# ScalarE copies P1's bank into P2's, and the second level of the ff residual's P5 and P7 in every block

## The chip, the cores and the metric

One NeuronCore of a Trainium2 chip runs the whole program. The metric is device time in microseconds (us) of one execution, lower is better. The engines meant below are TensorE (PE in the profile, PEld for its weight loads), VectorE (DVE), ScalarE (ACT), GpSimd (POOL) and SyncE (SP, which issues most DMAs).

## The reference, cut to what matters

Two sequences of 2048 rows with 512 features pass through one conditioned layer; everything is fp32.

```
emb = silu(t) @ ada_w + ada_b             # 6 rows of 512 per sequence: shift, scale, gate, twice
norm = LN(x) * (1 + scale_msa) + shift_msa
h = gelu(norm @ ssm_w1 + ssm_b1)          # 512 x 512, exact gelu
x = x + gate_msa * (h @ ssm_w2 + ssm_b2)  # 512 x 512
norm2 = LN(x) * (1 + scale_mlp) + shift_mlp
hf = gelu(norm2 @ ff_w1 + ff_b1)          # 512 x 1024, tanh gelu
x = x + gate_mlp * (hf @ ff_w2 + ff_b2)   # 1024 x 512
```

## The kernel before, in words

The 4096 rows are cut into eight blocks of 512 (`NBLK`), four to a sequence (`PER_B`), numbered 0 to 7. The gates are multiplied into the second weights, which is why those weights are folded anew for the second sequence (in the iteration of block 3 and what follows it, "refold").

Matrix products are done by Strassen's method (Winograd's form): 2 by 2 quarters, seven products P1 to P7 instead of eight, with sums of the operands ahead of them and sums of the results behind. Four kinds of products, in the order in which one iteration `i` of the main loop runs them:

- **products** (`Second.products`, tiles `hC_i`): hidden layer of the ff part of block i, a bilinear program of 26 products that is read from a table (`HK_P`). Its banks in PSUM are first taken by ACT (L946) and then added by DVE (L949); gelu is on ACT (L927). It takes 22.45 us of PE.
- **oA_{i+1}** (`residual`, `group`): the ssm residual of the next block, seven products of 1.727 us, 12.09 us together. `group` writes the products in the order ORDER = P1, P2, P6, P5, P7, P3, P4. Products that share a result are accumulated in one bank: BANK puts P1, P6, P7, P4 in bank y, P2 in x, P5 and P3 in v. DVE reads a bank after each product (L697) and adds it into `x`. P6 accumulates on P1 in bank y, and so on, so that the result of P1 is contained in what is read later. Banks y and v are seeded with the bias row by an ACT copy (`seed`, L446).
- **oC_i** (`residual_in_leaves`): the ff residual of block i. P1 and P6 are done plainly (16 passes of 215.9 ns each); P2, P3, P4 by a second level of seven "leaves" each, of 0.447 us. Where `five` is true (blocks 2, 3, 5, 6, 7), P5 and P7 are done by leaves as well, and in blocks 1 and 4 plainly. Leaf r of all five products is done together, the leaf P1 being r=0; DVE adds it from PSUM into `x` (L795).
- **hA_{i+2}** (`First`, `hidden`): hidden layer of the ssm part of the block after next, again seven products in ORDER, results taken by DVE or, for those named in `on_act`, by ACT; gelu on ACT. In blocks with `five` those are P6 and P5, else none.

The operands of Strassen's products need sums: of the hidden values (L348, on POOL, mostly 128x512 or 128x256 tensor_tensor), of the normalised rows ("forms", L870, on POOL) and of the weights of the leaves (`leaves_of_weight`, L348). The last kind is made twice, for each sequence. In block 1 its parts for P2, P3, P4 are on POOL in products 1; the eight instructions for P5 and P7, called `later`, are on DVE (128x256), three in hA_3 and five in products 2. In block 4 all parts are on DVE, after the weights were multiplied by the gate.

The order is written out by hand. Each group of products calls `hooks`: a list of operations put behind each product (by name in `group`, by slot number in `products`, R0 to R6 for the leaves), and an engine runs its instructions in the order in which they are written. Nothing is scheduled by a tool. An operation in a hook thus stands in the queue of its engine in front of all that is written later, whether or not anybody waits for it.

Norm statistics are done on DVE (L508, L509, bn_stats), their scales in eight small POOL instructions (L517 to L535, some 3 us), normalisation on ACT (L549), the transpose on DVE (L560) and DMAs.

## Time and profile before

| | us |
|---|---|
| median of 3 runs (lowest, highest) | 589.98 (589.6, 590.53) |
| the profiled execution | 591.35 |
| its span | 589.2 |
| PE busy | 579.3 (98%) |
| DVE busy | 432.1 (73%) |
| POOL busy | 424.2 (72%) |
| ACT busy | 241.4 (41%) |

The profiled execution's time is 1.37 us above the median; the span is 2.15 us shorter than its own time. Times below are counted from the start of the span. PE starts and ends of stages that the text uses: oA_2 155.56, oC_1 167.65, products 2 202.93, oC_2 237.46, hA_5 329.16, products 4 341.25, oA_5 363.97, oC_4 376.06, products 7 537.72, oC_7 561.63; PE's last matmul ends at 585.17. In the list of instructions by time ("the timeline"), the columns are the start, the busy time, engine, line, operation, what is written from what, shapes, how many run together (x2 is two, with their common busy time), and in brackets the idle time of the engine before it with what ended it. In the list of waits, each line has the waiting instruction, the one waited for, and the total, the number and the longest of the waits.

### The profile page before, as it was taken

Reading aid. Unit: us, or ns where it says so; the run is one execution under the profiler, and the core shown is the slowest. Engines: PE = TensorE matmul, PEld = TensorE weight load, DVE = VectorE, ACT = ScalarE, POOL = GpSimd, SP = SyncE. Lnnn points to the kernel's source line nnn. Section 1 sums busy time; section 2 is a strip of 40 time slices with the busy share of each in tenths; the row PEclk is TensorE's granted clock in tenths of the full one; section 3 lists DMA queues with packets and bytes.
Section 4 is the critical chain, followed back from the end, with each engine's and each line's share of the span. In section 5 each row is a group of like instructions: output and inputs, shape, how many; then the busy total and the mean of one; then the engine's idle time right before and its main releaser. Section 6 shows DMA issues by size and latency. Waiting matters only on the chain.

```text
span 589.2 us, 9347 instructions
## 1 busy us (share of the span) xinstructions
PE 579.3 (98%) x3255; PEld 515.4 (87%) x3255; DVE 432.1 (73%) x784; ACT 241.4 (41%) x417; POOL 424.2 (72%) x509
## 2 busy tenths in 40 slices
PE   7999999999999999999999999999999999999997
PEld 3888888888889888998889988898889988898887
DVE  4979788987755785776757697767767736688686
ACT  2235357405633255434742457114464245322420
POOL 1776259999964958979788769965979792756461
PEclk9999999999999999999999999999999999999999
DMA  8990323403215402462033711423120420013002
GB/s 314 395 389 11 92 59 80 113 19 125 51 23 144 161 0 68 117 205 78 1 90 78 280 71 23 122 49 123 44 54 20 135 81 1 0 40 105 1 1 73
DMA packets 25243, 56.49 MB, mean 96 GB/s; under 512 B 4672, under 2 KB 5740, under 8 KB 23532
## 3 DMA queue, kind: packets, MB, share of 16 engines
q1 hardware_dynamic: 21472, 51.15, 27.3%
q10 hardware_dynamic: 3724, 4.75, 3.3%
q8 instruction: 26, 0.43, 0.3%
q14 instruction: 21, 0.17, 0.1%
HBM read 32.80 MB, written 8.40 MB: 70 GB/s over the span
## 4 chain that ended last, share of the span: by engine, by line
PE 89%; DVE 3%; DMA 2%; POOL 2%; issue 1%; ACTq 1%; ACT 0%; SPq 0%; POOLq 0%; DVEq 0%
PE px_hC L932 10%; PE py_hA L474 9%; PE py_oA L474 9%; PE pv_hC L932 8%; PE py_hC L932 8%; PE py_oC L735 7%; PE pl_oC_P_y L781 6%; PE pv_hA L474 4%; PE pv_oA L474 4%; PE pl_oC_P_v L781 4%; PE py_hC L474 2%; PE px_hA L474 2%; PE px_oA L474 2%; PE py_oC L474 2%; DMA ada<-in_L_cond_ada_w_dram 2%; PE pl_oC_P_x L781 2%
## 5 line engine op out<-in xcount | busy, mean ns | idle before, releaser
L508 DVE BATCH_NORM_STATS2 st<-x 128x6 f32<-128x512 f32 x64 | 43.4, 678 | 6.6 <-DMA x<-in_x_dram 6.4
L348 POOL TENSOR_TENSOR hSC<-hClo,hChi 128x512 f32<-128x512 f32 (+1 forms) x17 | 20.6, 1214 | 37.9 <-ACT hChi L927 19.1
L592 ACT ACTIVATE nT<-nT,mod,mod 128x512 f32<-128x512 f32 x30 | 22.0, 802 | 61.2 <-DMA nT<-blocks 46.5
L870 POOL TENSOR_TENSOR forms<-forms 128x256 f32<-128x256 f32 x55 | 41.4, 752 | 4.7 <-DVE forms L870 1.5
L932 PE MATMUL py_hC<-forms,fw 128*128 128x256 f32 x168 | 40.8, 379 | 0.0
L949 DVE TENSOR_TENSOR hClo<-hClo,py_hC 128x512 f32<-128x512 f32 x42 | 28.6, 684 | 15.4 <-ACT hClo L946 8.6
L549 ACT ACTIVATE nT<-x,nmr,rstd 128x512 f32<-128x512 f32 x32 | 23.4, 803 | 33.3 <-POOL nmr L535 33.3
L932 PEld LDWEIGHTS py_hC<-forms,fw 128*128 128x128 f32 x168 | 31.8, 190 | 4.4
L697 DVE TENSOR_TENSOR x<-py_oA,x 128x512 f32<-128x512 f32 x32 | 22.0, 688 | 18.1 <-PE py_oA L474 16.8
L795 DVE TENSOR_TENSOR x<-pl_oC_P_y,x 128x256 f32<-128x256 f32 (+1 forms) x76 | 28.1, 371 | 9.6 <-PE pl_oC_P_y L781 7.7
L592 ACT ACTIVATE x<-x,mod,mod 128x512 f32<-128x512 f32 x24 | 17.6, 802 | 39.7 <-DMA x<-blocks 39.7
L735 PE MATMUL py_oC<-fw,hClo 128*128 128x256 f32 x144 | 33.5, 379 | 0.0
L870 POOL TENSOR_TENSOR forms<-nT 128x256 f32<-128x256 f32 x12 | 8.9, 742 | 29.9 <-DMA out_dram<-x 10.2
L735 PEld LDWEIGHTS py_oC<-fw,hClo 128*128 128x128 f32 x144 | 26.7, 190 | 3.3
L870 POOL TENSOR_TENSOR forms<-nT,forms 128x256 f32<-128x256 f32 x39 | 28.7, 755 | 1.0 <-DVE forms L870 0.5
L517 POOL TENSOR_SCALAR ve<-mv 128x4 f32<-128x4 f32 x16 | 3.8, 240 | 34.3 <-DVE mv L509 26.1
L949 DVE TENSOR_TENSOR hChi<-hChi,pv_hC 128x512 f32<-128x512 f32 x35 | 23.2, 679 | 7.1 <-PE pv_hC L932 7.0
L927 ACT ACTIVATE hClo<-hClo,colsT 128x256 f32<-128x256 f32 x56 | 25.3, 499 | 6.0 <-DVE hClo L949 5.7
L932 PE MATMUL px_hC<-forms,fw 128*128 128x256 f32 x112 | 27.6, 379 | 0.0
L474 PE MATMUL py_oA<-w,hA 128*128 128x256 f32 x112 | 26.5, 379 | 0.0
L927 ACT ACTIVATE hChi<-hChi,colsT 128x256 f32<-128x256 f32 x56 | 25.1, 497 | 1.9 <-DVE hChi L949 1.9
L946 ACT ACTIVATE hClo<-px_hC 128x512 f32<-128x512 f32 x21 | 12.5, 597 | 32.0 <-PE px_hC L932 25.4
(330 smaller groups left out, 1763.5 us busy)
## 6 DMA issues: line engine op xcount, KB each, us to landing
x<-in_x_dram SPq DMA_DIRECT2D x13, 1024.0 KB
out_dram<-x SPq DMA_DIRECT2D x14, 512.0 KB
ada<-in_L_cond_ada_w_dram SPq DMA_DIRECT2D x6, 1024.0 KB
x<-blocks SPq DMA_DIRECT2D x96, 64.0 KB
nT<-blocks SPq DMA_DIRECT2D x72, 64.0 KB
fw<-in_L_cond_ff_w_dram SPq DMA_DIRECT2D x2, 2048.0 KB
nT<-blocks ACTq DMA_DIRECT2D x56, 64.0 KB
w<-in_L_cond_ssm_w_dram SPq DMA_DIRECT2D x3, 1024.0 KB
```

The source lines that it names most:

```text
L474: nc.tensor.matmul(ps[b][j * apart][:, j, :], lhs(p, j, k), rhs(p, j, k), start=(fresh and j * (not apart) == 0 and k == 0), stop=(p in (" ...
L508: nc.vector.bn_stats(st, xs[self.i][:, c, :])
L549: nc.scalar.activation(t, x_c, AF.Identity, bias=self.nmr[:, c : c + 1], scale=self.rstd[:, c : c + 1])
L592: nc.scalar.activation(dst, src, AF.Identity, bias=shift, scale=scale)
L697: nc.vector.tensor_tensor(d, ps[BANK[p]][:, js], d, ALU.add)
L735: yield lambda j=j, k=k: nc.tensor.matmul(ps[BANK[p]][:, j, :], hops(p, j, k), wops[p][:, k, :], start=False, stop=(k == kdim - 1), skip_g ...
L781: nc.tensor.matmul(t[:, n, :], hops.leaves[p][f][:, k, :], leaf_wops[p][f][:, k, :], start=room not in started, stop=(f in ("P2", "P3", "P ...
L795: nc.vector.tensor_tensor(d, src, d, ALU.add)
L870: eng.tensor_tensor(reg[d], reg[a], reg[b], ALU.add if f == "+" else ALU.subtract)
L927: nc.scalar.activation(h, h, AF.Gelu_apprx_tanh, bias=fb1T[:, m : m + 1])
L932: nc.tensor.matmul(ps[b][:, j, :], fa[ra][:, j * P : (j + 1) * P], fb[rb].rearrange("p a (c q) -> p c a q", q=Q), start=(fresh and j == 0) ...
L949: nc.vector.tensor_tensor(dest(d), dest(d), ps[b], op)
```

## The change

- A second order, CARRIED = P1, P5, P6, P2, P7, P3, P4, is used in residual oA_2 to oA_7 and in hidden hA_3 to hA_7. After P1, ACT copies P1's bank y into bank x, PSUM to PSUM (128x512), and P2 accumulates on the copy. DVE no longer adds P1 on its own; in hA, ACT takes the finished bank x by gelu with the bias. The hooks stay at their positions: the place is that of ORDER (`places`). P6, which writes bank y next, now waits for the copy. `on_act` is P6 and P5 in all of these hA.
- In oC of blocks 1 to 5 and 7 the same is done one level down: after leaf r=0, ACT copies P23's y bank (128x256), P4's y bank (128x256) and the v seed (128x128) into the x banks on which leaf P2 (r=1) accumulates, and DVE's four adds of r=0 are dropped.
- `five` is true in every block, so P5 and P7 are done by leaves in blocks 1 and 4 too, with their sums on POOL.
- `later` of block 1 moves into oA_2: two DVE instructions behind each of its first four products. `apart_leaves` moves from oC to slot 4 of products 1 and 4.
- The refold for the second sequence is spread in another way: seven folds and P23 sums in hA_5, POOL sums of 128x1024 at slots 5 and 8 of products 4, the P4 leaf sums on POOL, P23's last two and two of `later` on DVE in oA_5, the other six of `later` in oC_4.
- The statistics of norm 1 of block 6 move from DVE to ACT: four Identity activations with an accumulated sum in hA_5 and four Square activations in products 4.
- Block 7: `sums24` on DVE, `sums35` and `sums7` on POOL; leaf r=6 in the order P4, P7, P2 and P3, P5. Block 6: the adds of r=5 in the order P5, P4, P7, P3.

```diff
+    CARRIED = ("P1", "P5", "P6", "P2", "P7", "P3", "P4")
@@ group
+            if p == "P1" and order is CARRIED:
+                ps["x"] = [ps_g.tile([P, 2, HT], F32, tag="x", name=f"px_{name}_0")]
+                nc.scalar.copy(ps["x"][0], ps["y"][0])
-            for op in hooks.get(p, ()):
+            for op in hooks.get(place, ()):
@@ Norm
+        def sums_on_act(self):
...
+                nc.scalar.activation(
+                    self.unread[:, c], xs[self.i][:, c, :], AF.Identity, scale=1.0 / D, accum_out=self.mv[:, c, :1]
+                )
+        def squares_on_act(self):
...
+                nc.scalar.activation(
+                    self.unread[:, c], xs[self.i][:, c, :], AF.Square, bias=less[:, c : c + 1], accum_out=self.mv[:, c, 1:]
+                )
@@ hidden
             if p == "P1":
-                take_first(p, s1, ps["y"], 0)
+                if order is not CARRIED:
+                    take_first(p, s1, ps["y"], 0)
+            elif p == "P2" and order is CARRIED:
+                for j in range(2):
+                    nc.scalar.activation(s1[:, j], ps["x"][:, j], func, bias=bT[:, m0 + j : m0 + j + 1])
@@ residual
+            if p == "P1" and order is CARRIED:
+                return
@@ residual_in_leaves
+            if last and r == 6:
+                on = ("P4", "P7", "P2", "P3", "P5")
...
+            if r == 0 and carried:
+                x23, x4 = rooms["P23", "x"], rooms["P4", "x"]
+                nc.scalar.copy(x23[:, :2], rooms["P23", "y"][:, :2])
+                nc.scalar.copy(x4[:, : 1 + five], rooms["P4", "y"][:, : 1 + five])
+                if five:
+                    nc.scalar.copy(x4[:, 2], seeded[:, 0])
+                started |= {("P23", "x"), ("P4", "x")}
+                dests = {}
+            for p in ("P5", "P4", "P7", "P3") if i + 2 == NBLK and r == 5 else on:
@@ main loop, products
-        five = i % PER_B != (1 if i < PER_B else 0)
+        five = True
-            hook(hooks, (0, 1, 3, 5, 7), later)
+            hook(hooks, (1, 1, 3, 5, 7), unread_stats)
-            hook(hooks, (0, 0, 1), fold[:3])
-            hook(hooks, (9,), fold[3:7])
+            hook(hooks, (0,), fold[:1])
+            hook(hooks, (5, 8), fold[1:5])
+            hook(hooks, (8, 13), fold[5:7])
+            hook(hooks, (13,), fold[9:13])
+            hook(hooks, (4,), [lambda: apart_leaves(gb[5], nc.gpsimd)])
@@ main loop, oA and oC
-        engs = (nc.gpsimd, nc.gpsimd, nc.gpsimd if nx2 else nc.vector)
+        engs = (nc.vector if last else nc.gpsimd, nc.gpsimd, nc.gpsimd if nx2 or last else nc.vector)
+            if i == 1:
+                hook(hooks, ("P1", "P1", "P2", "P2", "P6", "P6", "P5", "P5"), later)
-                hook(hooks, ("P1", "P2", "P6", "P5"), fold[7:11])
+                hook(hooks, ("P1", "P2", "P6", "P5"), fold[8:9] + fold[7:8] + later[:2])
-            residual(f"oA_{i + 1}", i + 1, hA[i + 1], w2_ops, KD // 2, hooks)
+            residual(f"oA_{i + 1}", i + 1, hA[i + 1], w2_ops, KD // 2, hooks, order=CARRIED)
+            hook(hooks, ("P1", "R0") if leaf_fold else ("P1", "P1", "R0") if nx2 else ("P1",), [lambda c=c: n2[i + 1].normal(c) for c in range(C)])
+                hook(hooks, ("P1",), leaf_fold[2:])
@@ main loop, hA
-            hook(hooks, ("P5", "P5", "P7", "P3", "P4"), fold[:5])
+            hook(hooks, ("P5", "P5", "P5", "P7", "P7", "P3", "P4"), fold[:7])
-            hook(hooks, ("P1", "P2", "P6"), later[:3])
-            st = n1[i + 3].stats()
+            st = n1[i + 3].sums_on_act() if refold5 else n1[i + 3].stats()
+            unread_stats = n1[i + 3].squares_on_act() if refold5 else []
-            hook(hooks, ("P7", "P4") if refold5 else ("P5", "P7", "P3", "P4"), st[:2] if refold5 else st)
+            hook(hooks, ("P7", "P7", "P4") if refold5 else ("P5", "P7", "P3", "P4"), st)
-            hA[i + 2] = First(i + 2, n1[i + 2].ops, hooks, on_act=("P6", "P5") if five else ())
+            hA[i + 2] = First(i + 2, n1[i + 2].ops, hooks, CARRIED, on_act=("P6", "P5"))
```

## The prediction

> **What bounds the kernel now.** I read the page first, then the chain that ended last, then PE's waits.
>
> ```profile
> PE 579.3 (98%) x3255; PEld 515.4 (87%) x3255; DVE 432.1 (73%) x784; ACT 241.4 (41%) x417; POOL 424.2 (72%) x509
> PEclk9999999999999999999999999999999999999999
> PE 89%; DVE 3%; DMA 2%; POOL 2%; issue 1%; ACTq 1%; ACT 0%; SPq 0%; POOLq 0%; DVEq 0%
> PE pv_hC L932 <- POOL forms L870: 1.2, 1, 1.2
> PE pl_oC_P_y L781 <- POOL forms L348: 0.6, 1, 0.6
> ```
>
> PE is the bound: 98% busy at a full clock, and after the start it waits twice, 1.2 us at 539.97 and 0.6 at 573.74. So only three things can gain: fewer PE passes, those two waits, and what follows the last matmul. Work taken off DVE gains nothing by itself, since PE never waits for it in oA or hA; but any new lateness of another engine is lost time. So I looked next at the stages that change, first oC in blocks 1 and 2 (time of the stage, then busy time and count by engine), then each engine's timeline where new work is placed.
>
> ```profile
> 167.65:190.84 23.19, 23.19 (x150) 21.54 (x148) 13.54 (x31) 7.51 (x11) 11.22 (x18) 1.00 0.34 92
> 237.46:260.00 22.54, 22.54 (x174) 21.71 (x173) 17.84 (x41) 8.97 (x14) 17.05 (x23) 1.00 0.51 146
> ```
>
> The first column shows the price of `five`: 23.19 without, 22.54 with it.
>
> **The change, part by part.** The sum is made against the profiled execution, 591.35, which is 1.37 over the median of 589.98.
>
> Gain 1, leaves in blocks 1 and 4: P5 and P7 each go from 16 passes of 215.9 ns (3.455) to 28 of 111.7 (3.128). Four products save 4 x 0.327 = 1.31; the two stages above give the same, 2 x 0.65. **-1.31**.
>
> Gain 2, the wait at 539.97. It ends with a read by DVE of bank v, though the view names POOL:
>
> ```profile
> 538.16 1.60 DVE L795 TENSOR_TENSOR x<-pl_oC_P_v,x 128x256 f32<-128x256 f32 x4
> 539.68 0.41 DVE L795 TENSOR_TENSOR x<-pl_oC_P_y,x 128x256 f32<-128x256 f32 x1
> ...
> 538.32 3.14 POOL L870 TENSOR_TENSOR forms<-forms 128x256 f32<-128x256 f32 x4 [1.49 <-DVE forms L870]
> 541.42 0.72 POOL L870 TENSOR_TENSOR nT<-nT,forms 128x256 f32<-128x256 f32 x1
> ```
>
> The last of four adds of 0.40 ends at 539.76. With P3 put last, the banks that PE needs come free 0.4 earlier. But the product at 541.77 waits for POOL's form of 541.46, so only some 0.2 of it stays. **-0.2** (0 to -0.4).
>
> Gain 3, the wait of 0.6 in oC_7 for POOL's sums: half of them move to DVE, at 1.1 to 1.5 each (the rows of oC_7 below), from 565.3 on; done near 570, before 573.7. **-0.57** (0 to -0.6).
>
> Gain 4, the tail: after the last matmul DVE runs two adds of together 0.75 (585.21 to 585.96), then the DMA is issued. In the new leaf order one of 0.42 is left. **-0.33** (0 to -0.4).
>
> Dropping DVE's reads of P1 (11 of 0.69) and of r=0: **0**, as PE did not wait for them.
>
> Cost 1, `later` in oA_2. In oA_2 DVE idles 0.96 to 1.10 between its adds, so two instructions of 0.42 would fit. But a DVE tensor_tensor with both inputs in SBUF does not take 0.42 beside a POOL tensor_tensor. In oC_7 both engines' rows stand side by side:
>
> ```profile
> 565.89 1.08 DVE L348 TENSOR_TENSOR forms<-hClo 128x256 f32<-128x256 f32 x1
> 567.01 1.38 DVE L348 TENSOR_TENSOR forms<-forms,hClo 128x256 f32<-128x256 f32 x1
> 568.31 1.48 DVE L348 TENSOR_TENSOR hClo<-hClo 128x256 f32<-128x256 f32 x1
> 569.71 1.49 DVE L348 TENSOR_TENSOR forms<-hClo,forms 128x256 f32<-128x256 f32 x1
> 571.12 0.41 DVE L795 TENSOR_TENSOR x<-pl_oC_P_y,x 128x256 f32<-128x256 f32 x1
> ...
> 566.77 1.33 POOL L348 TENSOR_TENSOR forms<-forms,hSC 128x512 f32<-128x512 f32 x1
> 568.07 1.44 POOL L348 TENSOR_TENSOR hSC<-hSC 128x512 f32<-128x512 f32 x1
> 569.47 1.45 POOL L348 TENSOR_TENSOR forms<-hSC,forms 128x512 f32<-128x512 f32 x1
> ```
>
> Each DVE instruction ends 0.28 after a POOL one ends (568.10 and 568.39; 569.51 and 569.79), so they go at POOL's pace, one per 1.40; an add from PSUM is not slowed. POOL is busy back to back from 139.16 to 167.28, all of oA_2, and gets 0.4 more ahead of it from `apart_leaves`. The POOL sum that starts at 155.94 then ends at 157.6, so the first `later` ends at 157.9, the second at 159.3. Behind each add of DVE stand two more. The eighth ends at 157.9 + 7 x 1.40 = 167.7, and the add of P7, which is queued behind it, at 168.4. P4 writes P7's bank and waits for that add; due at 165.92, it starts at about 168.55. Of this, 0.4 is lost earlier, where P7 waits for the read of P6 (162.75). **+2.6**. Lower bound 0, if they take 0.42; with the mean pace of those four rows, (571.12 - 565.89) / 4 = 1.31, it is 1.9; upper bound 3.0, with 1.46 a piece.
>
> [...]
>
> Cost 2, ACT's queue at hA_5 and products 4. There, in CARRIED, the gelu of P2 and its table load of 1.28 come after P2 (6.9 into hA) and not at the start; 128x512 statistics at 0.80 each (0.72 start to start, the row L549) come on top, and ACT takes the first banks of products 4 behind them. From the table load at 336.2: load 1.28, two gelus 0.9, gelu of P7 to 339.4, two statistics to 340.9, gelu of P3 to 341.5, two of P4 to 342.4, two statistics to 343.8, two takes of 0.60 to 344.9, a Square to 345.6, the next take to 346.2. In the trace the corresponding takes are here:
>
> ```profile
> 342.31 1.09 ACT L946 ACTIVATE hChi<-py_hC 128x512 f32<-128x512 f32 x2
> 344.04 0.60 ACT L946 ACTIVATE hChi<-px_hC 128x512 f32<-128x512 f32 x1 [0.64 <-PE px_hC L932]
> ```
>
> PE wants the second bank of px_hC again at 345.56, with 0.93 to spare now; with the take at 346.2 it waits about 0.7. DVE's adds after it have 0.06 and 0.28 to spare at two places, which a shift of both by the wait does not use. **+0.8** (0 to 1.6, the upper end with two more ACT instructions of 0.80 in front).
>
> Cost 3, waits for the copies. No row copies PSUM to PSUM; the nearest are PSUM to SBUF 0.60 (L946) and SBUF to PSUM 0.58 (L446); bounds 0.37 (0.58 + 0.60 less SBUF to SBUF 0.80) and 0.80. I take 0.58. In blocks 2, 3, 5 ACT ends the gelus of hC 2.63 after oA starts (228.0); the copy would end at 3.25, P6 is due at 3.46. In block 4 it may wait 0.1. Leaf copies: in block 2 the scales end 6.44 into oC, two normalisations 8.0, the copy of P23 8.4; leaf P2 is due at 9.14. So 0.1 for the copies and 0.2 for oC_4, where six of `later` on DVE delay the transposes and hence the leaf adds. **+0.3** (0 to 1.5).
>
> Costed at **0**, with the cover. The same move of the table load in hA_3, 4, 6 and 7: ACT idles 3.1 to 5.6 ahead of L656 there (in hA_6 it is busy until 405.1, still 1.0 ahead of P2's end), and ends the gelus of P4 13.1 into hA, beside 13.0 for the first bank of products (in the trace ACT takes that bank 1.1 after it is full, and PE has 1.3 to spare); if that cover went, cost 2 would come again, 0.7 each. The new POOL sums: in block 1 POOL idles 3.75 from 167.28 on, and the five-product blocks run the same sums without a PE wait. POOL's refold sums in products 4: its chain of scales starts 9.5 into the stage by the reckoning above, beside 10.7 now, so the two added leaf sums of 0.73 each still let hSC start near 364.40, as now; late, they would hold up the leaves of oC_4, which have over 2 us. The copies on ACT in hA end 0.7 after P1 and are wanted 1.7 after it; in hA_6 the four L592 that hold ACT now until 403.2, 3.9 into the stage, would hold up the copy by 1.0, but the transposes ahead of them move from 14.5 into oC_4 to 8, and they should end ahead of hA_6. No DMA queue gets another order.
>
> Sum: -1.31 - 0.2 - 0.57 - 0.33 + 2.6 + 0.8 + 0.3 = +1.29. The profiled execution would be 592.6, its median 591.3.
>
> **The rivals.** (A) Contention in oA_2 does not bite: DVE does `later` at 0.42 in its gaps. For it: the same eight took 6.2 in all in hA_3 and products 2, 0.77 each. Against it: POOL has no gap here. Without cost 1: 588.7; without costs 2 and 3 too: 587.6. It decides below a pace of 1.2: the stall is then under 1.3 and no loss is left. This is the case on the other side.
>
> (B) ACT is late in every block: a copy of 0.80 and late normalisations hold up P6 and leaf P2. For it: the gaps of 0.2 and 0.7 are small and occur in four or five blocks. Against: ACT is 41% busy. At 0.2 to 0.6 a block and costs 1 and 2 at their upper ends, about +2.7 more: 594.
>
> (C) Leaves that do not pay, as sums come late in blocks 1 and 4: 1.31 less gain, 592.6. Against it: the same sums in block 2 cause no wait.
>
> **How the numbers follow.** A run's times spread by 0.2%, 1.2 us, which no change could be told from. The likeliest case has 0.5, own range 589.9 to 592.8; A 0.25 (587.6 to 589.6); B 0.17; C 0.08. The range 588.3 to 594.0 leaves out the ends of A and B. Faster than 588.8: most of A, 0.17. Slower than 591.2: a bit over half of the likeliest, B and C, 0.51. Between: 0.32.
>
> **What would show it.** In the changed profile: oC_1 and oC_4 of 22.5 us; DVE's L348 in oA_2 at 1.1 to 1.5 with a PE wait of about 2 us on DVE's add of P7; a PE wait on L946's successor in products 4; one DVE add after PE's end; no wait at oC_7. I am wrong if DVE's `later` run at 0.42, or if PE waits for the new copies in most blocks.

## The result, and the profile after

| | before | after |
|---|---|---|
| median of nine runs each (lowest, highest) | 590.19 (589.6, 592.45) | 593.36 (592.51, 595.88) |
| ratio after to before, 95% interval | | 1.0056 (1.0038 to 1.0073) |
| the profiled execution | 591.35 | 594.65 |
| its span | 589.2 | 592.9 |

The changed kernel is slower by 3.2 us, about 0.6%. The profiled execution of after is 1.29 over its median, that of before 1.16 over its own.

From the page of the changed kernel, first the busy time of each engine, then the clock by slice, then the shares of the chain that ended last:

```profile
PE 582.0 (98%) x3303; PEld 517.3 (87%) x3303; DVE 415.1 (70%) x750; ACT 261.9 (44%) x477; POOL 434.4 (73%) x522
...
PEclk9999999999989999999999999999999999999999
...
PE 83%; DVE 8%; DMA 4%; issue 1%; POOL 1%; ACTq 1%; ACT 1%; SPq 0%; DVEq 0%; POOLq 0%
```

The change did what it says with the work: DVE lost 17 us, ACT gained 20, POOL 10. PE issues 48 matmuls more, each with a weight load (leaves are smaller and more numerous), and is busy 2.7 us longer, although the leaves alone should have saved it 1.31. The second row says most of why: one slice, the twelfth, has an 8 where before every slice had a 9. PE ran part of it at a lower clock (in experiment 1, at full clock, PE is busy for 579.7). In the chain DVE's share went from 3% to 8%.

PE's waits in the changed kernel (waiting instruction, the one waited for, total us, number, longest):

```profile
PE py_oA L475 <- DVE x L735: 2.3, 2, 1.9
...
PE py_hC L981 <- DVE forms L919: 1.1, 1, 1.1
PE pv_hC L981 <- POOL forms L919: 0.6, 1, 0.6
PE py_hC L981 <- DVE hClo L998: 0.4, 1, 0.4
```

The wait of 0.6 in oC_7 is gone. The one at the start of products 7 is now two, together 1.7 instead of 1.2. New are two waits in oA_2 for DVE's adds, and one in products 4. A wait here is idle time of PE; a stage loses some 0.25 more than that (in experiment 4 a wait of 2.24 costs its stage 2.50), which is called restart below.

I compared the start of every stage on PE in the two traces. This table has all stages that moved by more than 0.1, and oC_1, for which a gain was forecast; every other stage took the same time within that:

| stage | after minus before, us | the prediction's term |
|---|---|---|
| start of the span up to oA_2 | -1.56 | none: code that is the same in both |
| oA_2 | +3.90 | cost 1, +2.6 |
| oC_1 | -0.02 | half of gain 1, -0.65 |
| products 4 | +0.71 | cost 2, +0.8 |
| oC_4 | -0.22 | half of gain 1 and cost 3, -0.65 + 0.2 |
| oC_6, up to the start of products 7 | +1.13 | none |
| products 7 | -0.14 | gain 2, -0.2 |
| oC_7 | -0.67 | gain 3, -0.57 |
| after the last matmul | +0.50 (4.06 to 4.56) | gain 4, -0.33 |
| sum | +3.63 | span 592.86 less 589.23 |

The first row is no effect of the change. In before's profile the first product of block 0 starts at 16.55, in after's at 14.76, and in every later profile but that of experiment 9, also of kernels made from before, 1.4 to 1.9 earlier than in before's: its profiled execution began late. Without that row the two profiled executions differ by 4.86 us (594.65 less 591.35, and 1.56), more than the medians do; 1.69 of it is a fall of PE's clock in oA_2 and oC_1, shown below, which not every execution has. In the nine executions of after the mean clock goes from 1.000 to 0.994; the four longest (594.21, 594.46, 594.65 and 595.88) have 0.996, 0.997, 0.996 and 0.994, the median one (593.36) has 1.000. Without the clock too, 3.17 is left, which is also the difference of the medians.

The largest row is oA_2. DVE and PE there in the changed kernel, by time (start, busy time, engine and line, what is written from what, idle time ahead with its releaser in brackets):

```profile
158.32 1.07 DVE L348 TENSOR_TENSOR fw_s<-fw_s 128x256 f32<-128x256 f32 x1
159.31 1.49 DVE L348 TENSOR_TENSOR fw_t<-fw_s,fw_t 128x256 f32<-128x256 f32 x1
160.73 0.68 DVE L735 TENSOR_TENSOR x<-py_oA,x 128x512 f32<-128x512 f32 x1
...
163.54 0.68 DVE L735 TENSOR_TENSOR x<-px_oA,x 128x512 f32<-128x512 f32 x1
...
164.96 1.48 DVE L348 TENSOR_TENSOR fw_t<-fw,fw_t 128x256 f32<-128x256 f32 x1
166.37 0.68 DVE L735 TENSOR_TENSOR x<-py_oA,x 128x512 f32<-128x512 f32 x1
...
161.55 1.97 PE L475 MATMUL py_oA<-w,hA 128*128 128x256 f32 x8 [0.48 <-DVE x L735]
...
167.10 3.09 PE L475 MATMUL py_oA<-w_s,hA 128*128 128x256 f32 x8 [1.86 <-DVE x L735]
```

The reader is to see two things. `later`'s instructions (the L348 rows of DVE) take up to 1.49 (the eight 0.42 to 1.49, 1.12 in the mean), and the add of P7 at 166.37 stands behind the last of them; P4 waits 1.86 for it. The adds at 160.73, 163.54 and 166.37 are 2.81 and 2.83 apart, with two of `later` between them, where a product takes 1.73. And the eight passes of P4 then take 3.09, where the same eight at 161.55 took 1.97. The next view shows why, the same stretch cut into windows (from:to, length, then busy time and count of PE, PEld, DVE, ACT, POOL, granted clock, share of the DMA engines and GB/s):

```profile
164.00:167.00 3.00, 1.24 (x6) 0.76 (x4) 3.00 (x5) 2.52 (x4) 3.00 (x3) 1.00 0.00 0
...
168.00:171.00 3.00, 3.00 (x9) 2.37 (x8) 1.33 (x4) 0.21 (x1) 2.35 (x4) 0.50 0.00 0
...
172.00:175.00 3.00, 3.00 (x20) 2.75 (x19) 1.91 (x5) 0.00 (x0) 1.43 (x3) 1.00 0.00 0
```

After a window in which PE was busy for 1.24 of 3.00 us, the granted clock is 0.50 for 3.4 microseconds (167.84 to 171.25), and PE gets 9 passes done where it gets 20 later. So the wait costs twice: 2.34 us of idle time and what follows, and then half speed for a while. Of that, 1.05 lies in oA_2 and 0.64 in oC_1, which loses here what its leaves gain.

### The profile page after: what moved, and what is told of

The parts are those of the page before. It is cut to its first block, busy times and chain, and to the rows that moved or that the text cites. A ratio compares the mean times of both kernels' runs of the same rounds, so it can differ in the third digit from the quotient of the medians.

```text
span 592.9 us, 9491 instructions
## 1 busy us (share of the span) xinstructions
PE 582.0 (98%) x3303; PEld 517.3 (87%) x3303; DVE 415.1 (70%) x750; ACT 261.9 (44%) x477; POOL 434.4 (73%) x522
## 4 chain that ended last, share of the span: by engine, by line
PE 83%; DVE 8%; DMA 4%; issue 1%; POOL 1%; ACTq 1%; ACT 1%; SPq 0%; DVEq 0%; POOLq 0%
PE px_hC L981 9%; PE py_hA L475 9%; PE py_oA L475 8%; PE py_hC L981 7%; PE py_oC L774 7%; PE pv_hC L981 7%; PE pl_oC_P_y L820 6%; PE pv_hA L475 4%; PE pl_oC_P_v L820 4%; PE pv_oA L475 4%; PE py_oC L475 2%; PE py_hC L475 2%; DMA ada<-in_L_cond_ada_w_dram 2%; PE pl_oC_P_x L820 2%; PE px_oA L475 2%; PE px_hA L475 2%
## 5 line engine op out<-in xcount | busy, mean ns | idle before, releaser
L348 POOL TENSOR_TENSOR hSC<-hClo,hChi 128x512 f32<-128x512 f32 (+1 forms) x17 | 20.4, 1207 | 42.1 <-ACT hChi L976 24.7
L512 DVE BATCH_NORM_STATS2 st<-x 128x6 f32<-128x512 f32 x60 | 40.6, 676 | 5.1 <-DMA x<-in_x_dram 4.8
L591 DVE STREAM_TRANSPOSE blocks<-nT 128x512 f32<-128x512 f32 x32 | 22.3, 707 | 18.8 <-ACT nT L580 18.8
L834 DVE TENSOR_TENSOR x<-pl_oC_P_y,x 128x256 f32<-128x256 f32 (+1 forms) x66 | 24.7, 375 | 2.4 <-PE pl_oC_P_y L820 0.9
L735 DVE TENSOR_TENSOR x<-py_oA,x 128x512 f32<-128x512 f32 x26 | 17.8, 686 | 11.8 <-PE py_oA L475 11.3
L774 PE MATMUL py_oC<-fw,hClo 128*128 128x256 f32 x112 | 26.0, 386 | 0.0
L697 DVE TENSOR_TENSOR hA<-py_hA,hA 128x512 f32<-128x512 f32 x7 | 4.8, 690 | 30.0 <-PE py_hA L475 19.2
L774 PE MATMUL py_oC<-fw_s,hSC 128*128 128x256 f32 x112 | 25.3, 379 | 0.0
```

Source lines behind the costliest of these rows:

```text
L512: nc.vector.bn_stats(st, xs[self.i][:, c, :])
L591: nc.vector.transpose(self.bl[:, :, :, c, :].rearrange("p m k q -> p k m q"), self.nT[:, c, :].rearrange("p (k m q) -> p k m q", k=KD, m=C),)
L774: yield lambda j=j, k=k: nc.tensor.matmul(ps[BANK[p]][:, j, :], hops(p, j, k), wops[p][:, k, :], start=False, stop=(k == kdim - 1), skip_g ...
L834: nc.vector.tensor_tensor(d, src, d, ALU.add)
```

## The experiments

Eleven kernels, each run beside the kernel before on the same chip. Experiments 5 to 9 and 11 start from experiment 1. The first two take the large row of the table apart.

**1. `later` spread.** The changed kernel, with only four of the eight `later` in oA_2, one behind a product, and the other four in oC_1, where POOL has no large sums to do.

```diff
-                hook(hooks, ("P1", "P1", "P2", "P2", "P6", "P6", "P5", "P5"), later)
+                hook(hooks, ("P1", "P2", "P6", "P5"), later[:4])
@@ oC
+            if i == 1:
+                hook(hooks, ("P1",), later[4:])
```

> The changed kernel, with one of the eight later sums on DVE behind each of oA_2's first four products instead of two, and the other four behind P1 of oC_1, where POOL idles 3 us. Theory (DVE at POOL's pace): one sum of 1.4 and one add of 0.6 fit into a product of 1.73, so both PE waits of oA_2 (0.48 and 1.86) go: -2.3. Theory (the clock falls because PE waited): the stretch at clock 0.50 from 168 to 172 goes too, another -2.0: -4.4 in all, to about 589.0. Rival (clock falls for another reason, heat or load): only -2.3, and the stretch stays. Rival (DVE simply has too much to do in the stage): the waits shrink with the number of sums, not go, and come back in oC_1.

Measured: 590.09 against 589.72, ratio 1.0007 (0.9998 to 1.0017); profiled 590.12, span 588.3, mean clock 1.000. oA_2 takes what it took before, without a wait, and oC_1 is 0.65 shorter. The rest stands: products 4 +0.71, oC_4 -0.23, oC_6 +1.36, products 7 -0.15, after the last matmul 4.55.

DVE's row of one of the four that were moved, and of a sum that matters below, in experiment 1 (columns as above):

```profile
170.18 0.41 DVE L348 TENSOR_TENSOR fw_t<-fw 128x256 f32<-128x256 f32 x1
...
347.69 2.00 DVE L348 TENSOR_TENSOR fw_t<-fw 128x512 f32<-128x512 f32 x1
```

Beside POOL's small scale instructions (128x4) such an instruction takes 0.41 to 0.42 (all four in oC_1), beside POOL's sums of 128x512 in oA_2 0.47 to 1.55. At 0.42, two would fit into each of the gaps of 0.96 to 1.10 that DVE has there. What follows: where `later` stands is worth some 2.9 us of the median (ratio 1.0056 to 1.0007), nearly the whole loss. All else in the change comes out within 0.2% of zero.

**2. `later` alone.** The kernel before with only those eight instructions put into oA_2. (Block 1's plain P5 and P7 then read weights that `later` has already overwritten, so those products are computed from other numbers; the instructions and their shapes are the same.)

```diff
+            if i == 1:
+                hook(hooks, ("P1", "P1", "P2", "P2", "P6", "P6", "P5", "P5"), later)
+                later = []
```

> The kernel before, with only the eight later sums moved into oA_2, two behind each of its first four products. Theory (contention and clock): P7's add on DVE ends some 2.5 late, as P1's add of 0.69 is in DVE's queue here too; PE waits 2.3 to 3.0 in oA_2, and the clock falls to one half behind it: +2.3 to +5.0 against before. Rival (the waits of oA_2 come from the new order of products, not from the sums): 0.

Measured: 592.86 against 589.72, ratio 1.0056 (1.0041 to 1.0071); profiled 594.15, span 592.3. PE's waits in it:

```profile
PE py_oA L474 <- DVE x L697: 1.9, 2, 1.1
...
PE pv_hC L932 <- DVE hClo L949: 1.0, 1, 1.0
PE pv_oA L474 <- DVE x L697: 0.9, 1, 0.9
```

oA_2 is 3.47 longer. In ORDER three products wait, for 1.10, 0.85 and 0.77, where in CARRIED two wait for 0.48 and 1.86, and the clock does not fall. So the loss in oA_2 needs nothing else of the change; CARRIED only gathers it into fewer waits. The profile has another wait of 1.0 in products 5 (+1.31), at 434.31, far from the edit. DVE's read stands there behind a transpose that hangs, by way of a normalisation, on POOL's scales; POOL comes to these 1.9 later into the stage than in before; it makes its forms from block 6's modulations, and those begin 1.65 late (see experiment 3). This execution is 1.29 above the median, so the others may not have that wait.

**3. The copies alone.** The kernel before with CARRIED in oA and hA, the leaf copies in blocks 2, 3, 5 and 7 and the normalisations that go with them, and nothing else of the change. (Blocks 1 and 4 keep their old leaves, and part of what is accumulated on the copies is probably overwritten, so the output is another; the instructions and their order are those that are timed.)

> The kernel before with the new order and the ACT copies alone: CARRIED in oA_2 to oA_7 and hA_3 to hA_7, the leaf copies in blocks 2, 3, 5 and 7 with normalisations 3 and 4 behind them, P6 and P5 taken by ACT in all hA. Statistics, later, refold and the last block as before; blocks 1 and 4 without the leaves of P5 and P7. Theory (DVE's reads of P1 were hidden, the copies are hidden too): 0, within 0.5, and no PE wait on a copy. Rival (the copies are late): +0.2 to +0.6 in each of blocks 2, 3, 5, together +1 or more, with PE waits on the copies in oA or at leaf P2.

Measured: 591.29 against 589.72, ratio 1.0028 (1.0017 to 1.0039); profiled 591.89, span 590.1. No wait on a copy was expected. In oA and in the leaves there is none; the whole loss is one wait in hA:

```profile
PE py_hA L475 <- ACT px_hA L489: 2.3, 1, 2.3
```

ACT's rows at that place, the start of hA_6:

```profile
400.15 2.93 ACT L596 ACTIVATE nT<-nT,mod,mod 128x512 f32<-128x512 f32 x4 [14.24 <-DVE st L512]
402.99 0.57 ACT L489 COPY px_hA<-py_hA 128x512 f32<-128x512 f32 x1
```

The copy stands in ACT's queue behind four modulations, which wait for the transposes; P6, which writes the bank that is copied, waits for the copy. hA_6 takes 2.57 longer, every other stage the same as before within 0.2. (For the first row the view names DVE as the releaser, in before the DMA of the transposed rows.) In the changed kernel the same place has:

```profile
399.92 2.93 ACT L623 ACTIVATE nT<-nT,mod,mod 128x512 f32<-128x512 f32 x4 [8.92 <-DVE x L834]
403.99 0.57 ACT L489 COPY px_hA<-py_hA 128x512 f32<-128x512 f32 x1 [1.13 <-PE py_hA L475]
```

There ACT has idled 1.13 when P1 is done: block 6's transposes come earlier (their transfers are issued from 391.78 on, in before from 393.08 on, although this stage starts 2.8 us later in after's profile). So copies cost nothing in themselves, at 0.57 for 128x512; they cost what stands ahead of them in the queue.

The wait is longer than before's trace would give. In both kernels the transfers are issued 6.17 ahead of the start of hA_6 (399.25 in before, 397.75 here), but the modulations begin 0.98 after that start in before (400.23) and 2.40 after it here. One thing differs: as hA_6 starts and the last of these transfers end, at 397.75, a packet of code comes. The view of the DMA queues from 397 to 399 has it (queue, packets, MB, share):

```profile
q8 instruction: 1, 0.02, 3.4%
```

Before has none there. Neither has experiment 4, and its modulations begin at 0.96; experiment 2 has one 0.01 after the start of hA_6, and they begin at 2.63. No run was made to test this place; experiments 8 and 10 test such packets at another.

**4. Doses of waiting.** To find what makes the clock fall, the kernel before with 4, 5, 6 and 7 idle statistics on DVE behind P5 of oA_2, oA_3, oA_4 and oA_6. They delay DVE's adds and so PE; nothing reads them.

```diff
+            dose = {1: 4, 2: 5, 3: 6, 5: 7}.get(i, 0)
+            spare = small.tile([P, nc.vector.BN_STATS_DIM], F32, tag="spare", name=f"spare_{i}", bufs=1)
+            hook(hooks, ("P5",), [lambda: nc.vector.bn_stats(spare, xs[i + 1][:, 0, :]) for _ in range(dose)])
```

> The kernel before, with 4, 5, 6 and 7 spare statistics of 0.7 (DVE, results unused) behind P5 of oA_2, oA_3, oA_4 and oA_6, so that PE waits for DVE's add of P7 by about 1.1, 1.8, 2.5 and 3.2. Theory (a wait of some 2 us makes the clock fall to one half for some 4 us): the granted clock stays 1.00 behind the first, and falls to 0.5 behind the last two at the least, each costing another 2: +8.6 of waits and +4 or more of clock. Rival (the fall behind the wait of 1.86 was chance or belongs to the leaves): no fall, +8.6 alone.

Measured: 600.92 against 589.72, ratio 1.0189 (1.0168 to 1.0209); profiled 600.98. The four waits are 0.78, 1.51, 2.24 and 2.96. Windows at the end of the third, in the fourth, and after it (columns as for the windows above):

```profile
308.00:312.00 4.00, 3.27 (x15) 2.91 (x16) 3.39 (x7) 2.87 (x5) 2.75 (x4) 1.00 0.09 30
...
448.00:451.00 3.00, 0.24 (x2) 0.00 (x0) 2.90 (x5) 2.06 (x3) 2.92 (x4) 0.91 0.10 22
453.00:457.00 4.00, 4.00 (x11) 3.12 (x10) 1.94 (x4) 0.00 (x0) 0.00 (x0) 0.50 0.00 0
```

The clock stayed at 1.00 after the first three, of which the third was expected to make it fall, and fell to 0.50 at the last, for 6.83 us. The first three stages lost 1.05, 1.78 and 2.50, each its wait and 0.27; the fourth 4.98 and 1.24 more in the stage behind it, so 3.0 over its wait and the 0.27. Single waits of 2.24 here and 2.33 in experiment 3 had no such price, nor had 1.10, 0.85 and 0.77 within six microseconds in experiment 2. But 1.86 with 0.48 five microseconds earlier had it in the changed kernel, and so had 1.00 and 1.15 close together in experiment 10, and 2.97 in experiment 6. There is thus no one length of wait here from which the clock falls, nor one sum of waits, and what decides it stays open. The time at half clock was 3.41 us in the profiles of after and of experiments 6 and 10, and 6.83, twice that, in this one. In after the longer wait was 1.86, and PE was busy for 1.24 of the 3.00 us around it.

**5. The tail: sums earlier.** Experiment 1 with all of block 7's `sums24` behind P1, on the theory that DVE comes late to the last adds because of them.

```diff
-            hook(hooks, ("P1",), sums24[:2])
-            hook(hooks, ("P6",), sums24[2:])
+            hook(hooks, ("P1",), sums24)
```

> The kernel with the later sums spread (the first experiment), and all four of block 7's sums24 on DVE behind P1 instead of two behind P1 and two behind P6. Theory (the end is late because DVE is behind: two sums of 0.68 stand in front of the leaf adds and DVE never catches up): what follows the last matmul falls from 4.55 to about 3.7, as only one add of 0.42 is left there; -0.9. Rival (the new order of the last leaves itself makes the adds bunch): 4.4 to 4.6, no change.

Measured: 590.40 against 589.93, ratio 1.0012 (1.0001 to 1.0024); profiled 590.44, span 588.6. The theory fell: DVE's last add starts 0.12 after PE ends, as it does in the changed kernel, and what follows the last matmul (the tail) is still 4.55. The last issues, first of the changed kernel, then of experiment 5:

```profile
588.42 0.42 DVE L834 TENSOR_TENSOR x<-pv_oC,x 128x256 f32<-128x256 f32 x1
588.88 0.38 SPq L884 DMA_DIRECT2D out_dram<-x  x1
588.88 0.46 ACTq L884 DMA_DIRECT2D out_dram<-x  x1
```

```profile
584.19 0.42 DVE L834 TENSOR_TENSOR x<-pv_oC,x 128x256 f32<-128x256 f32 x1
584.64 0.38 SPq L884 DMA_DIRECT2D out_dram<-x  x1
584.65 0.46 ACTq L884 DMA_DIRECT2D out_dram<-x  x1
```

And of the kernel before:

```profile
584.94 0.38 SPq L835 DMA_DIRECT2D out_dram<-x  x1
585.21 0.75 DVE L795 TENSOR_TENSOR x<-pl_oC_P_y,x 128x128 f32<-128x128 f32 x2 [0.29 <-PE pl_oC_P_y L781]
585.99 0.38 ACTq L835 DMA_DIRECT2D out_dram<-x  x1
```

In the new order of leaf r=6 the last add completes both halves of the output at once, and both transfers, of 128 KB each, start together; before, one started 1.05 ahead of the other. The last add ends 0.54 after PE's end in after and 0.79 in before. Against that, the last packet of output ends 1.94 after the last issue (588.88 to 590.82) instead of 1.48 (585.99 to 587.47), and from there to the last instruction of the program it is 2.04 instead of 1.76.

**6. Statistics back on DVE.** Experiment 1 with block 6's norm 1 statistics on DVE, as before the change.

```diff
-            st = n1[i + 3].sums_on_act() if refold5 else n1[i + 3].stats()
-            unread_stats = n1[i + 3].squares_on_act() if refold5 else []
+            st = n1[i + 3].stats()
+            unread_stats = st[2:] if refold5 else []
...
-            hook(hooks, (1, 1, 3, 5, 7), unread_stats)
+            hook(hooks, (7, 9), unread_stats)
```

> The kernel with the later sums spread, and the statistics of norm 1 of block 6 on DVE again, two in hA_5 and two at slots 7 and 9 of products 4. Theory (ACT's statistics cost 0.3 of the 0.71 lost in products 4, DVE's sum at slot 13 the other 0.5): products 4 loses 0.3 less, if DVE has room for 1.4 more, else as much again; -0.3 to +0.5. Rival (the recorded one: ACT's queue costs all of it): -0.7.

Measured: 594.3 against 589.93, ratio 1.0076 (1.0046 to 1.0105). Products 4 is 5.12 longer than before, with this wait and a clock fall after it:

```profile
PE pv_hC L981 <- DVE hClo L998: 3.0, 1, 3.0
```

With the refold's P23 sums and the statistics both on it, DVE reads the banks of products 4 three microseconds late. ACT's eight activations are what the rest of the change needs, and at +0.71 they are the cheaper side. oC_4 is the full 0.65 shorter in this run, without a wait for a copy.

**7, 11. The wait in products 4.** In the changed kernel products 4 waits twice: 0.09 for ACT, after which a product starts 0.25 late, and 0.40 for a read by DVE, after which one starts 0.56 late (the number in the expectations). With the restart they cost 0.32 and 0.66. The kernel before lost 0.27 at another product of this stage (22.72 in all, 22.45 in products 5), and that is gone; so the stage is 0.71 longer. ACT's rows there:

```profile
338.63 1.28 ACT L688 ACT_TABLE_LOAD   x1 [0.93 <-PE px_hA L475]
...
341.67 0.61 ACT L524 ACTIVATE unread<-x 128x512 f32<-128x512 f32 x1
342.19 0.19 ACT L524 ACTIVATION_READ_ACCUMULATOR unread<-x 128x1 f32 x1
...
345.72 1.08 ACT L995 ACTIVATE hChi<-py_hC 128x512 f32<-128x512 f32 x2
346.67 0.73 ACT L535 ACTIVATE unread<-x,less 128x512 f32<-128x512 f32 x1
347.38 0.61 ACT L995 ACTIVATE hChi<-px_hC 128x512 f32<-128x512 f32 x1
```

The first wait is what the prediction reckoned: the take of px_hC at 347.38 stands behind a Square. For the second I suspected the P23 sum on DVE at slot 13. Experiment 7 is experiment 1 with that sum at slot 10:

```diff
-            hook(hooks, (8, 13), fold[5:7])
+            hook(hooks, (8, 10), fold[5:7])
```

> The kernel with the later sums spread, and the second P23 sum on DVE at slot 10 of products 4 instead of 13. Theory (the sum in front of the read of bank py_hC holds up PE by 0.56 at slot 16): that wait goes, products 4 loses some 0.2 instead of 0.71; -0.5. Rival (ACT's queue costs it): 0.

Measured: 591.2 against 589.93, ratio 1.0026 (1.0011 to 1.0042). Products 4 is 1.34 longer than before, with a wait of 1.02 in place of 0.40: the sum now stands ahead of the same read. So it was not the sum at slot 13 that made it late, but something ahead of both. oC_4 is 0.65 shorter, without the wait for the copy.

The row at 347.69 of experiment 1, shown above, is that something: the first P23 sum, 128x512 on DVE, took 2.00, because POOL runs this beside it:

```profile
346.79 2.36 POOL L348 TENSOR_TENSOR fw_s<-fw 128x1024 f32<-128x1024 f32 x1
```

Experiment 11 is experiment 1 with the first P23 sum at slot 6, `sums24` as in experiment 5, and the old order of leaf r=6:

```diff
-            if last and r == 6:
-                on = ("P4", "P7", "P2", "P3", "P5")
-            hook(hooks, (8, 13), fold[5:7])
+            hook(hooks, (6, 13), fold[5:7])
-            hook(hooks, ("P1",), sums24[:2])
-            hook(hooks, ("P6",), sums24[2:])
+            hook(hooks, ("P1",), sums24)
```

> The kernel with the later sums spread, and three more edits in two stages. Block 7: all four sums24 behind P1 and the leaf r=6 in the old order, so that DVE is not behind and only one transfer is left at the end; what follows the last matmul falls from 4.55 to 4.0 (as in the kernel before), if these two are the causes, and stays over 4.3 if not. Products 4: the first P23 sum on DVE at slot 6 instead of 8. Theory (that sum, issued beside a POOL sum of 2.36, takes 2.00 and holds up the three adds behind it, which is the PE wait of 0.56): it takes 0.7 to 1.2 at slot 6, the wait goes, products 4 loses 0.3 instead of 0.71. Rival (slot 13's sum is the cause): 0.71 stays. In all 589.2, against 589.7 to 590.0 of the kernel before.

Measured: 590.17 against 589.84, ratio 1.0002 (0.9992 to 1.0012); profiled 589.73, span 587.9. Its DVE row for that sum:

```profile
346.37 0.80 DVE L348 TENSOR_TENSOR fw_t<-fw 128x512 f32<-128x512 f32 x1
```

0.80 and not 2.00, and products 4 is within 0.04 of before, although the wait of 0.08 for ACT is still there. But the gain does not reach the end. Its one new wait is this:

```profile
PE pl_oC_P_x L820 <- ACT pl_oC_P_x L852: 1.1, 1, 1.1
```

ACT's rows ahead of it:

```profile
383.10 0.81 ACT L580 ACTIVATE nT<-x,nmr,rstd 128x512 f32<-128x512 f32 x1 [6.44 <-POOL nmr L566]
383.82 0.36 ACT L852 COPY pl_oC_P_x<-pl_oC_P_y 128x256 f32<-128x256 f32 x1
```

PE waits for the leaf copy in oC_4, which is now 0.88 longer than before instead of 0.23 shorter. The copy stands behind a normalisation, for which ACT idles 6.44, and its releaser is the last of the scales, on POOL. POOL is busy without a break from 341.5 on up to that scale, and the copy runs at 383.82 here and at 383.17 in experiment 1: later, though PE comes to it earlier. (With the sum at its new place POOL's sum of 128x1024 starts at 347.45, in experiment 1 at 346.79.) So in block 4 it is POOL that sets the time, and what PE gains ahead of it is given back there. The tail is 4.36 with the old leaf order, over the 4.3 that the expectation names as the sign that its two causes are not the cause: the two transfers are again 1.0 apart (583.36 and 584.40) and the last packet ends 1.50 after its issue, much as in before, but from there to the last instruction it is still 2.05. So the leaf order is worth 0.19 of the 0.50; the rest belongs to something else in the changed kernel and stays open.

**8, 9, 10. Products 7: the same code at other places of the program.** oC_6 and the start of products 7 took 1.13 longer in after, 1.36 in experiment 1, though no engine has more to do there. DVE's and POOL's forms, for which PE waits, come from transposed rows, and the 16 transfers that carry those, half of them on ACT's queue, are slow to issue. First the kernel before, then after (start, busy time, queue, what is written, eight issues together):

```profile
526.36 5.57 ACTq L569 DMA_DIRECT2D nT<-blocks  x8
```

```profile
529.12 6.80 ACTq L600 DMA_DIRECT2D nT<-blocks  x8
```

In the view of the DMA queues the changed kernel has, between 530.5 and 533.5, one packet of 16 KB on the queue that carries instructions:

```profile
q8 instruction: 1, 0.02, 2.7%
```

In the kernel before this queue has no packet between 523 and 532; one comes in the window 532 to 535, behind the burst. There are 26 such packets in before and in after, for 6510 and 6606 matmuls and weight loads of PE, one to some 250, and 27 in experiment 9 with 6706. So the packets seem to carry PE's instructions, and where they fall depends on how many PE has had. The theory: a packet that meets the burst lengthens it. Experiment 8 is experiment 1 with the idle matmuls at the start split, 15 more of them (60 instructions on PE), which do no other work; experiment 10 is the same edit to the kernel before; experiment 9 shifts by 100 places with 29 small matmuls, and has the old order of r=6.

```diff
-    warm(IDLE - 1, C)
+    warm(C * (IDLE - 1), 1)
-    warm(1, C)
+    warm(C, 1)
```

> The kernel with the later sums spread, and at its start, where PE waits for the first loads, 15 more matmuls (20 of 128 columns for 5 of 512, results unused), so that PE's instructions all stand 60 places later. Theory (the 1.36 lost ahead of products 7 comes from a packet of 16 KB of instructions on queue 8, which falls into the 16 transfers of block 7's transposed rows and holds up both issuing queues by 1 us): the packet comes some 4 us earlier, ahead of these transfers; the issues take 5.0 to 5.6 as in the kernel before instead of 6 to 7, and the loss goes; -1.3. Rival (the transfers are late for another reason, such as what else moves then): no change.

> The kernel with the later sums spread, the leaf r=6 of block 7 in the old order (P2, P3, P5, P4, P7), and 29 small matmuls instead of 4 wide ones at the start, so that PE's instructions stand 100 places later. Theory on the end (in the new order the last add completes the rows of both queues' last transfers, so two of 128 KB go out after it instead of one): what follows the last matmul falls from 4.55 to 4.0, -0.5. Rival: it stays. Theory on the code packets (queue 8): they fall some 7 us earlier, ahead of both tight bursts of transfers (59 to 64 and 524 to 531), so products 7 loses nothing and hC_0 has no wait: -1.4. Rival: the losses stay or move. In all -1.9, to about 588.2, which would be 1.5 to 2 under the kernel before.

> The kernel before, with nothing but 15 more matmuls at its start (20 of 128 columns for 5 of 512, results unused), PE's instructions 60 places later. Theory (code packets hold up the transfers that they meet): the packet of queue 8 at 534 comes at about 530 and meets the transfers of 526 to 532; their issue takes 6 to 7 instead of 5.6 and products 7 starts some 1.2 later: +1.2, up to +2 if an early burst is met too. Rival (the delay belongs to the changed kernel): 0.

Measured: experiment 8, 590.69 against 589.93, ratio 1.0006 (0.9993 to 1.0018), profiled 590.35, span 588.6. Experiment 10, 594.31 against 589.77, ratio 1.0077 (1.0063 to 1.0091), profiled 593.99, span 591.9, clock 0.997. The same burst, experiment 8 first, then 10:

```profile
526.23 5.29 ACTq L600 DMA_DIRECT2D nT<-blocks  x8
```

```profile
526.33 6.17 ACTq L569 DMA_DIRECT2D nT<-blocks  x8
```

In experiment 8 the packet falls at 525.4, ahead of the burst; the issue takes 5.29, and the stretch is 0.16 shorter than before instead of 1.36 longer. In experiment 10, where the only edit is 60 idle instructions at the start, the packet falls at 530.8, in the burst; the issue takes 6.17, products 7 starts 1.00 later, and with two waits close together the clock falls and takes 1.68 more. Both shifted kernels pay at another place as well: a packet at 61.1 meets the burst of block 0 (seven issues on ACT's queue take 5.94 and 5.79 where they took 4.60), and products 0 loses 1.24 and 1.16. Experiment 8 loses another 0.50 in products 3 and oA_4, experiment 10 0.62 in products 5. So the same edit gained at one place and lost at others, and experiment 8's total did not move.

The thirteen profiles together say the same of this burst. In seven (after and experiments 1, 5, 6, 7, 10 and 11) a packet falls into it; its issue on ACT's queue takes 6.17 to 7.22, and oC_6 is 0.73 to 1.58 longer than before. In the other six, before among them, none does; it takes 5.29 to 5.57, and oC_6 is at most 0.16 shorter than in before.

Experiment 9: 598.35 against 589.77, ratio 1.0156 (1.0122 to 1.0191). It says little by its time, for the small matmuls were not cheap: 58 passes of 64 columns took 0.22 us each, 12.6 in all, and the start alone lost 5.9 against before's profile, which began late itself. But oC_6 is 0.16 shorter there too, which agrees with experiment 8, and the tail, with the old order of r=6, is 4.36 as in experiment 11, where 4.0 was expected.

No version beat the kernel before: experiments 1, 8 and 11 can't be told from it.

## Why the prediction was right, and where not

It gave 591.3 in a range of 588.3 to 594.0, with slower the likeliest sign. The median is 593.36, slower by more than the 0.2% that can be told: in the range, but 2 us above the predicted time and nearer the upper end. By its steps:

- **What bounds the kernel.** Right. Work taken off DVE (17 us) moved nothing; every term that counted is one of PE's passes, one of its waits, its clock, or what follows the last matmul.
- **Gain 1, leaves, -1.31.** The size is right: oC_1 is 0.65 shorter in experiment 1, oC_4 in experiments 6 and 7. In the changed kernel only 0.24 of it is seen, 0.64 being eaten by the low clock in oC_1 and 0.43 by two late leaves in oC_4 (cost 3). Rival C, sums too late for the leaves, did not come about.
- **Gain 2, -0.2.** Its own part is about right: products 7 is 0.14 shorter, as bank v comes free earlier (its product starts 1.73 into the stage, 2.25 in before). What failed is that nothing else was reckoned ahead of products 7: oC_6 is 1.13 longer. The 48 more matmuls and their weight loads also moved the fetches of code, and one fell into the burst of transfers. The trace of before shows those packets, and the prediction left them out.
- **Gain 3, -0.57.** Right: the wait is gone, oC_7 is 0.67 shorter.
- **Gain 4, -0.33.** Wrong in sign: +0.50. One add is left after the last matmul, as the step says, and it ends 0.25 sooner after PE. What the step left out is what that add releases: both transfers now start with it, and the last packet ends 0.46 later after its issue. The other 0.28 lies between that packet and the last instruction; it stays with the old leaf order (experiments 9 and 11), and its cause is open.
- **Cost 1, `later`, +2.6.** The mechanism is right and shown (experiments 1 and 2), down to the two places, 0.48 at P7 and 1.86 at P4. The pace taken, 1.40 a piece, is right for two of `later` and the add between them (2.81 and 2.83); the rows of `later` alone are 1.12 in the mean, because the add, which the step counted at nothing, fills the rest. Waits and restart are 2.85, beside 2.6. What was left out is that PE's clock can fall after such a wait: oA_2 lost 3.90, 1.05 of it clock, and oC_1 0.64 more. The trace of before, with a full clock in every slice, has no row for it, but its price is missing also from the range's upper bound of 3.0. The median execution does not have this fall.
- **Cost 2, ACT at products 4, +0.8.** The number, 0.71, came out by luck. The wait for ACT is there, but it costs 0.32 and replaces a loss of 0.27 that the kernel before had in this stage: the take behind the Square ends 4.43 into the stage, where the step has 4.95; the statistics start 0.61 to 0.70 after each other, where 0.72 was taken. The other 0.66 is for DVE's slow P23 sum beside POOL (experiment 11: +0.04 without it). That DVE's sum would be slowed there follows from the same rows as cost 1; I used them in oA_2 only.
- **Cost 3, copies, +0.3.** About right: nothing in blocks 2, 3 and 5 and in hA, 0.43 in oC_4: 0.24 at leaf P2, which waits for a copy, and 0.19 at a later leaf on bank v, not on a copy. The copy of 128x512 takes 0.575, where 0.58 was taken. Rival B, ACT late in every block, did not come about.
- **Costed at zero, hA_6.** The prediction named the cover, earlier transposes, and 1.0 as the price without it. Experiment 3 takes the cover away, and the wait comes, as named, but at 2.57. The step took its 1.0 from before's trace, where the modulations begin 0.98 after the start of hA_6; in experiment 3 they begin 1.42 later than that, and a packet of code comes there as their transfers end. That this packet is the reason is read from four profiles and not tested.
- **Rival A**, no contention, is refuted by the rows of oA_2. With the contention taken away, in experiment 1, the gain that it forecast (588.7, 1.3 faster) does not come either: the ratio is 1.0007, because oC_6, products 4 and the tail took it back.

So the sign was right for the reason given. The profiled execution is 2.0 above the one forecast (594.65 and 592.6): the clock is 1.7 of it, oC_6 1.1, the tail 0.8, the other terms together 0.3; against these 3.9 stand 1.56, for the start that was late in the execution that the sum was made from, and 0.3 that lies outside the span (2.12 in before, 1.79 in after). That late start made the forecast of the profiled execution look better than its steps were. The medians do not hang on it, nor on the clock: the median is 2.1 above the forecast, of which oC_6 is 1.1 and the tail 0.8.

## What to carry to other kernels

A moved instruction is priced by what runs beside it, not by its own row elsewhere: the sums of `later`, 128x256 on DVE from SBUF, took 0.41 to 0.42 us in oC_1 of experiment 1, without large sums on POOL, and 0.47 to 1.55 beside POOL's sums of 128x512 in oA_2. So put such sums where POOL has no large ones, and look at the engine's neighbour, not only at its gaps. Where PE is the bound, a wait can cost twice, because the clock may fall after it, by 1.7 to 3.0 us here; its length alone does not tell whether it will (1.86 after 0.48 had that price in after, a single 2.24 in experiment 4 had not). And a difference of 1 us far from the edit (oC_6 here, 1.13), in a stage whose work is the same, is to be looked for in the bursts of transfers and the instruction fetches that meet them, before a story is made of the edit.

## What was unexpected of the hardware

- The granted clock fell to 0.50 for 3.41 or 6.83 us: with 0.48 and 1.86 us of waiting five microseconds apart, with 1.00 and 1.15, and with a single 2.96 or 2.97, but not with a single 2.24 or 2.33.
- A burst of 16 transfer issues took longer where a 16 KB packet of code fell into it: 6.17 to 7.22 us on ACT's queue with it in seven profiles, 5.29 to 5.57 without it in six. Adding 15 matmuls at the start of the kernel before, which do nothing, made it slower by 0.77%.
- An ACT activation with an accumulated sum is followed by a read of the accumulator of 0.19 to 0.21 us, which hardly holds up the next: two Identity activations of 0.61 to 0.63 start 0.61 to 0.62 apart, two Squares of 0.71 start 0.70 apart.
- A DVE sum of 128x512 took 2.00 beside a POOL sum of 128x1024 and 0.80 ahead of it.
- The last packet of two output transfers of 128 KB that were issued together ended 1.94 us after the issue; of two issued 1.05 apart, 1.48 after the second.
